# Routing-weight scaling of the experts' transposed results: from ScalarE and SyncE's queue to Pool

## The chip, the core and the metric

The kernel runs on one core of a Trainium2 chip. Its engines run side by side: TensorE (PE in the profile, with its weight loads as PEld), VectorE (DVE), ScalarE (ACT), GpSimd (POOL) and SyncE (SP), which only asks for DMA transfers. Each engine takes its instructions in order; semaphores order engines against each other. The metric is the device time of one execution in microseconds; the median of several runs is given.

## The reference, cut to what matters

Each of 8 batches of 256 tokens is first multiplied by the adapter matrix chosen for it. A mixture-of-experts layer follows: a shared feed-forward network for all tokens, and 16 experts of which each token uses its two best, weighted. The result is added to the input.

```python
x1 = einsum('bsi,boi->bso', x, weight[adapter_ids])           # 2048 tokens x 1024
shared_out = (silu(g_s) * u_s) @ shared_w_down.T              # g_s, u_s = split(x1 @ shared_w_gate_up.T)
probs = softmax(x1 @ gate_w.T)                                # 16 experts
topk_vals, topk_idx = top_k(probs, 2)                         # divided by their sum -> combine
act = silu(g) * u                                             # g, u = split(x1 @ w_gate_up[e].T), 256 each
moe_out = sum over e of (act_e @ w_down[e].T) * combine[:, e]
out = x + moe_out + shared_out
```

Everything is float32. The change touches the multiplication by `combine`.

## The kernel before, in words

**Products.** Float32 matrices are split into a high part (fp32r, a cast on ScalarE, L88) and the rest (a subtraction on VectorE, L89), and each product is three matmuls (`mm3`, L139 to L141): high by high, high by rest, rest by high. Weights are loaded by SP into a staging tile `st` (four buffers), and split into `hl` (five buffers, and two more in the experts' stage), by `load_w` (L119).

**Stages.** The kernel computes the adapters' products for all batches, the first half of the shared network and the routing (to about 440 us), then the experts (about 440 to 740 us), then the second half of the shared network with the final sums. The routing sorts the tokens of each expert into a list; experts are run in order of their load, counted here from 0. Expert n has room for `CAPS[n]` tokens: 304, 296, 288, 288, 280, 280, 272, 272, 264, 264, 264 for the first eleven, and 256 for the last five. A rarely needed loop at the end handles tokens beyond that.

**One expert.** Pool gathers its tokens' rows from memory, 128 rows of 1 KB per request (L839): eight requests into two `yg` tiles (four buffers, so two experts' worth), and one or two into the small tile `yl`. VectorE transposes them (L226) into `tt`, and they are split into `yte`. PE computes gate and up (`expert_up`), ScalarE the silu (L865), VectorE the product with up (L866), and the result is split into `at`. Then PE computes the down product.

**The down product of the first eleven.** Where an expert has more than 256 tokens, `expert_down_columns` has PE produce the result turned, with features on partitions: eight blocks of 128 features by all tokens, each in a bank of its own (seven banks `acc` go round). ScalarE copies each block into the tile `raw[0]` (L920, 88 copies). VectorE turns it with two 32x32 block transposes into `raw[1]` (L922). There, partition 32a + i holds, for token 32t + i, the features 256a to 256a + 255, for each of the `nt` groups of 32 tokens (`nt` is 10 for the first two experts and 9 for the nine after them). ScalarE multiplies each group by the token's weight, a value per partition from `cwt[:, t, n]` (L928). SP asks for four stores to `os_d`, each of 32 partitions by `nt` pieces of 1 KB (L936). `raw[0]` and `raw[1]` are single buffers: the next expert's copies wait for this expert's transposes, and the next expert's transposes wait for this expert's stores. The last five experts use `expert_down`, whose copy out of the bank already scales (L895).

**The order of the work.** The order of instructions on each engine comes from a scheduler that follows the program's order and its own estimate of times. The program steers it with a list `between`: `load_w` takes one entry after each weight load, and the entry's instructions are placed after that load's split. The main loop calls, for each n: the gathers of expert n+2, `expert_up` of n+1 (four loads), `expert_out` of n (two loads, then the down product), and the transposes and splits of n+2. An expert's scaling is thus spread over the fourth, fifth and sixth load after its down product. On SP, a store that waits holds back the weight loads behind it.

Of the kernel before, what the change touches and what calls it, by code (L numbers as in the profile page):

```python
# [13 lines left out]
AF = mybir.ActivationFunctionType  # L14
ALU = mybir.AluOpType
AX = mybir.AxisListType

P = 128
# [23 lines left out]
def adapter_moe_kernel(ctx: ExitStack, tc: tile.TileContext, xT, x, itok, wc, gate, wgu, wd, sgu, sd, out):  # L42
    nc = tc.nc
# [35 lines left out]
    def bank():  # L79
        turn[0] += 1  # L80
        return banks[turn[0] % 7]

    last_cast, last_split, last_load = [None], [None], [None]
# [17 lines left out]
    between = []  # L101
# [36 lines left out]
    def mm3(ps, lhs, rhs, first, last):  # L138
        nc.tensor.matmul(ps, lhs[0], rhs[0], start=first, stop=False)  # L139
        nc.tensor.matmul(ps, lhs[0], rhs[1], start=False, stop=False)  # L140
        last_product[0] = nc.tensor.matmul(ps, lhs[1], rhs[0], start=False, stop=last).ins  # L141
# [32 lines left out]
    cwt = cpool.tile([P, ENTRIES // 32, 32], F32, tag="cwt", name="cwt")  # L174
# [730 lines left out]
    def expert_down_columns(n, at, w):  # L905
        m, rows, nt = CAPS[n], ROWS[n], ROWS[n] // 32
        ot, o = (r[:, :, :].rearrange("p c n -> p (c n)") for r in raw)
        ot = ot[:, : 8 * rows].rearrange("p (b t i) -> p b t i", b=8, i=32)
        o = o[:, : nt * 256].rearrange("p (t f) -> p t f", t=nt)
        for b in range(8):  # L910
            ps = bank()
            for fi in range(2):
                mm3(
                    ps[:, :m],
                    [w[fi][:, l, b * P : (b + 1) * P] for l in range(2)],
                    [at[:, l, fi, :] for l in range(2)],
                    fi == 0,
                    fi == 1,
                )
            nc.scalar.copy(ot[:, b], ps[:, :rows].rearrange("p (t i) -> p t i", i=32))  # L920
        for k in range(2):
            nc.vector.transpose(o[:, :, k * P : (k + 1) * P].rearrange("p t (b j) -> p b t j", b=4), ot[:, 4 * k : 4 * k + 4])  # L922

        def scaled(ts, end):
            def work():
                with tc.issue_after(last_cast[0]):
                    for t in range(nt)[ts]:
                        nc.scalar.activation(o[:, t], o[:, t], AF.Copy, scale=cwt[:, t, n : n + 1])  # L928
                if end:
                    store()  # L930

            return work

        def store():
            for a in range(4):
                nc.sync.dma_start(  # L936
                    os_d[ROW0[n] : ROW0[n] + rows, 256 * a : 256 * a + 256].rearrange("(t i) f -> i t f", i=32),
                    o[32 * a : 32 * a + 32],
                )

        between[:] = [None, None, None, scaled(slice(0, 3), False), scaled(slice(3, 6), False), scaled(slice(6, nt), True)]


    def segments(ix, ib):
# [45 lines left out]
    def expert_out(po, n, at):  # L990
        w = load_wd(expert_id(n))
        if CAPS[n] > MAIN:
            expert_down_columns(n, at, w)
            return
        for j in range(2):
            (nc.gpsimd if n > 13 else nc.sync).dma_start(os_d[ROW0[n] + j * P : ROW0[n] + (j + 1) * P, :], expert_down(po, at, w, j * P, cw[:, j, n : n + 1]))
# [32 lines left out]
    op = up.begin_work()  # L1029
# [186 lines left out]
    for n in range(E):  # L1216
# [14 lines left out]
        if n + 1 == E:  # L1231
# [3 lines left out]
            op = up.begin_work()  # L1235
# [163 lines left out]
```

## Time and profile before

| | us |
|---|---|
| median of 3 runs | 982.19 (979.61 to 986.2) |
| profiled execution | 981.36 |
| its span, from first to last instruction | 979.2 |
| PE busy | 962.2 |
| VectorE busy | 715.3 |
| ScalarE busy | 558.6 |
| of that, the scaling (L928, 101 x 497 ns) | 41.6 |
| Pool busy | 309.2 |
| of that, the gathers of rows into `yg` (L839, 128 x 1213 ns) | 155.2 |

Busy time is the time in which an engine executed an instruction; DMA requests count as busy on Pool, but not on SP. In a row of instruction groups stand the line, the engine, the operation, what it writes and reads, the count, then busy time and mean nanoseconds of one, then the idle time ahead of these instructions and what ended it. A row of a timeline has the start, the duration, the instructions, and in brackets the idle time before them.

### The profile page before, as it was taken

To read this page: it belongs to the slowest core of one execution; us is meant where nothing else is said; L and a number is where in the kernel's file an instruction comes from. 1 tells how busy PE (TensorE), PEld (TensorE's weight loads), DVE (VectorE), ACT (ScalarE), POOL (GpSimd) and SP (SyncE) were. 2 spreads that over 40 slices of the span, in tenths; PEclk is the share of its full clock that TensorE was granted. 3 is DMA by queue.
4 is the path that set the end of the run, shared out by engine and by line. 5 is a ranking of instruction groups with operands and counts; after the bars stand their busy time and mean duration, and the time that the engine had idled before them with its cause. 6 is when DMAs were issued, how large, how long until landed. Compare 5 with 4: busy or idle time off the path is not lost.

```text
span 979.2 us, 14565 instructions
## 1 busy us (share of the span) xinstructions
PE 962.2 (98%) x5183; PEld 834.5 (85%) x5183; DVE 715.3 (73%) x908; ACT 558.6 (57%) x819; POOL 309.2 (32%) x336
## 2 busy tenths in 40 slices
PE   8999999999999999999979999999999999999997
PEld 5888888888888888889969999999998888888886
DVE  4566888864779678649967888887878565969772
ACT  5556746566645452325758888878765465425440
POOL 2000200100074103666745556552001433330600
PEclk9999999999999999999979999999999999999999
DMA  8899967977799746868869989999997998994942
GB/s 299 283 322 356 372 209 278 370 252 246 247 213 259 164 126 134 295 233 260 243 221 286 309 279 287 299 308 321 310 328 263 326 355 310 272 263 127 250 147 100
DMA packets 92741, 257.62 MB, mean 263 GB/s; under 512 B 13298, under 2 KB 32514, under 8 KB 92658
## 3 DMA queue, kind: packets, MB, share of 16 engines
q1 hardware_dynamic: 60002, 173.04, 54.4%
q0 software_dynamic: 23056, 73.98, 23.9%
q10 hardware_dynamic: 9600, 9.57, 2.8%
q8 instruction: 42, 0.69, 0.3%
q14 instruction: 41, 0.34, 0.1%
HBM read 207.62 MB, written 48.93 MB: 262 GB/s over the span
## 4 chain that ended last, share of the span: by engine, by line
PE 94%; DMA 2%; issue 1%; DVE 1%; ACT 1%; SPq 0%; ACTq 0%
PE acc L530 31%; PE acc L141 19%; PE acc L139 19%; PE acc L140 19%; PE acc L731 5%; PE lp L286 1%; DMA st<-sd 1%; DMA st<-wc 1%; ACT hl L88 0%; DVE hl L89 0%; DVE shl L89 0%; ACT op L88 0%; DVE ca L759 0%; SPq L114 0%; DVE st L798 0%
## 5 line engine op out<-in xcount | busy, mean ns | idle before, releaser
L89 DVE TENSOR_TENSOR hl<-st,hl 128x1024 fp32r<-128x1024 f32 (+1 forms) x254 | 304.9, 1208 | 174.4 <-ACT hl L88 143.4
L88 ACT CAST hl<-st 128x1024 fp32r<-128x1024 f32 (+1 forms) x254 | 263.5, 1044 | 192.2 <-PE acc L141 70.6
L530 PE MATMUL acc<-op,hl 128*128 128x512 f32 x1296 | 298.0, 390 | 0.0
L530 PEld LDWEIGHTS acc<-op,hl 128*128 128x128 f32 x1296 | 242.4, 188 | 50.2
L839 POOL DMA_INDIRECT yg<-y_d,ix x128 | 155.2, 1213 | 80.1 <-issue 33.9
L141 PE MATMUL acc<-yte,hl 128*128 128x256 f32 (+6 forms) x512 | 147.2, 288 | 0.4 <-issue 0.4
L140 PE MATMUL acc<-yte,hl 128*128 128x256 f32 (+6 forms) x512 | 147.1, 287 | 0.3 <-issue 0.3
L139 PE MATMUL acc<-yte,hl 128*128 128x256 f32 (+6 forms) x512 | 147.3, 289 | 0.0
L140 PE MATMUL acc<-hl 128*128 128x512 f32 x256 | 100.3, 392 | 0.9 <-DVE hl L89 0.7
L141 PE MATMUL acc<-hl 128*128 128x512 f32 x256 | 99.7, 390 | 0.0
L141 PEld LDWEIGHTS acc<-yte,hl 128*128 128x128 f32 x512 | 96.3, 188 | 0.4 <-issue 0.4
L140 PEld LDWEIGHTS acc<-yte,hl 128*128 128x128 f32 x512 | 96.4, 188 | 0.2
L139 PEld LDWEIGHTS acc<-yte,hl 128*128 128x128 f32 x512 | 96.3, 188 | 0.2
L139 PE MATMUL acc<-hl 128*128 128x512 f32 x256 | 90.4, 391 | 1.5 <-ACT hl L88 1.5
L140 PEld LDWEIGHTS acc<-hl 128*128 128x128 f32 x256 | 48.0, 188 | 12.9 <-DVE hl L89 3.0
L139 PEld LDWEIGHTS acc<-hl 128*128 128x128 f32 x256 | 47.7, 188 | 12.3 <-ACT hl L88 2.5
L386 POOL DMA_INDIRECT tab_d<-tid,places x32 | 39.8, 1244 | 56.3 <-DVE ranks L372 46.8
L141 PEld LDWEIGHTS acc<-hl 128*128 128x128 f32 x256 | 48.1, 188 | 9.8
L139 PE MATMUL acc<-at,hl 128*128 128x264 f32 (+5 forms) x176 | 52.6, 299 | 2.7 <-issue 2.1
L141 PE MATMUL acc<-at,hl 128*128 128x264 f32 (+5 forms) x176 | 52.0, 295 | 2.5 <-issue 2.5
L140 PE MATMUL acc<-at,hl 128*128 128x264 f32 (+5 forms) x176 | 52.4, 298 | 1.3 <-issue 1.3
L141 PE MATMUL acc<-hl,ht 128*128 128x512 f32 x128 | 50.0, 391 | 0.0
(234 smaller groups left out, 1454.6 us busy)
## 6 DMA issues: line engine op xcount, KB each, us to landing
st<-wgu SPq DMA_DIRECT2D x64, 512.0 KB
st<-wc SPq DMA_DIRECT2D x63, 512.0 KB
st<-wd SPq DMA_DIRECT2D x32, 512.0 KB
st<-ss_d SPq DMA_DIRECT2D x30, 512.0 KB
st<-sd SPq DMA_DIRECT2D x30, 512.0 KB
st<-sgu SPq DMA_DIRECT2D x24, 512.0 KB
os_d<-raw SPq DMA_DIRECT2D x36, 288.0 KB
yr<-y_d POOLq DMA_DIRECT2D x20, 512.0 KB
```

The lines of the kernel that those rows point to most:

```text
L88: last_cast[0] = nc.scalar.copy(hi, src).ins
L89: last_split[0] = nc.vector.tensor_tensor(lo, src, hi.bitcast(F32), op=ALU.subtract).ins
L139: nc.tensor.matmul(ps, lhs[0], rhs[0], start=first, stop=False)
L140: nc.tensor.matmul(ps, lhs[0], rhs[1], start=False, stop=False)
L141: last_product[0] = nc.tensor.matmul(ps, lhs[1], rhs[0], start=False, stop=last).ins
L286: nc.tensor.matmul(lp[:, n0 : n0 + n], gpk[:, c * 2 * E : c * 2 * E + P], get(c)[l], start=(c == 0 and l == 0), stop=(c == NC - 1 and l == 1),
L386: i = nc.gpsimd.indirect_dma_start(out=tab_d[:, :], out_offset=bass.IndirectOffsetOnAxis(ap=places[r][:, tb : tb + 1], axis=0), in_=tid[r] ...
L530: last_product[0] = nc.tensor.matmul(ps, lhs[x], rhs[y], start=(first and c == 0 and i == 0), stop=(c == 3 and i == 2), skip_group_check=T ...
L731: nc.tensor.matmul(ps[k], lhs[x], rhs[y], start=(first and t == c == i == 0), stop=(t == c == 1 and i == 2), skip_group_check=True,)
L839: last_gather[0] = nc.gpsimd.indirect_dma_start(out=r[:, t * 256 : (t + 1) * 256], out_offset=None, in_=y_d.rearrange("k a p f -> (k a p) f"),
```

## The change

The three entries of `between` that scaled groups of 32 tokens on ScalarE become one entry, after the fourth load. It issues a single product on Pool: the whole of `raw[1]`, 128 partitions by `nt` x 256, times the weights spread over the 256 features by a stride of zero. The four stores are issued directly behind it by Pool instead of SP. Work, values and tiles are otherwise the same.

```diff
-        def scaled(ts, end):
-            def work():
-                with tc.issue_after(last_cast[0]):
-                    for t in range(nt)[ts]:
-                        nc.scalar.activation(o[:, t], o[:, t], AF.Copy, scale=cwt[:, t, n : n + 1])
-                if end:
-                    store()
-
-            return work
-
-        def store():
+        def scaled():
+            by = cwt[:, :nt, n : n + 1].to_broadcast([P, nt, 256])
+            nc.gpsimd.tensor_tensor(o, o, by, op=ALU.mult)
             for a in range(4):
-                nc.sync.dma_start(
+                nc.gpsimd.dma_start(
                     os_d[ROW0[n] : ROW0[n] + rows, 256 * a : 256 * a + 256].rearrange("(t i) f -> i t f", i=32),
                     o[32 * a : 32 * a + 32],
                 )
 
-        between[:] = [None, None, None, scaled(slice(0, 3), False), scaled(slice(3, 6), False), scaled(slice(6, nt), True)]
+        between[:] = [None, None, None, scaled]
```

Pool's instructions stand in one order with its gathers. In the changed program's order the first product stands behind the gathers of expert 5, the product of expert 3 behind those of expert 9, that of expert 6 behind those of expert 12, and that of expert 7 behind those of expert 14; between a product and its stores there are often one to five gathers. On VectorE the two transposes of an expert stand together and later than before, close to the point where the next expert's copies begin.

## The prediction

> **What bounds the kernel now.** I read the page first: busy shares, then the chain that ended last.
>
> ```profile
> PE 962.2 (98%) x5183; PEld 834.5 (85%) x5183; DVE 715.3 (73%) x908; ACT 558.6 (57%) x819; POOL 309.2 (32%) x336
> PE 94%; DMA 2%; issue 1%; DVE 1%; ACT 1%; SPq 0%; ACTq 0%
> ```
>
> TensorE is the bound: 98% busy, 94% of the chain. A change that relieves another engine can win only PE's idle time; one that makes another engine late costs at once. Pool's 32% is an average over stages, so next I read the experts' stage by stretches. The columns are PE, PEld, DVE, ACT and POOL busy, granted clock, DMA share and GB/s.
>
> ```profile
> 552.00:571.00 19.00, 19.00 (x152) 19.00 (x151) 16.31 (x19) 15.96 (x32) 11.16 (x10) 1.00 0.90 291
> 571.00:590.00 19.00, 19.00 (x153) 19.00 (x152) 16.05 (x19) 15.35 (x31) 10.25 (x10) 1.00 0.86 293
> 487.00:669.00 182.00, 174.76 (x1352) 172.75 (x1351) 149.06 (x165) 143.54 (x276) 102.83 (x87) 0.97 0.87 283
> ```
>
> One expert takes about 19 us and PE has no gap in it. PE's 7.2 us of idle time in the third row lie almost wholly at 489-500 and are put down to "issue", not to ScalarE. Next, Pool in time order, since the work goes there:
>
> ```profile
> 561.92 0.95 POOL L839 DMA_INDIRECT yl<-y_d,ix  x1 [3.52 <-DVE tt L226]
> 565.07 1.86 POOL L839 DMA_INDIRECT yg<-y_d,ix  x1 [2.19 <-DVE yte L89]
> 567.24 0.96 POOL L839 DMA_INDIRECT yg<-y_d,ix  x1 [0.30 <-issue]
> ...
> 575.74 0.96 POOL L839 DMA_INDIRECT yg<-y_d,ix  x1 [0.30 <-issue]
> 580.15 0.95 POOL L839 DMA_INDIRECT yl<-y_d,ix  x1 [3.46 <-DVE tt L226]
> 584.26 1.80 POOL L839 DMA_INDIRECT yg<-y_d,ix  x1 [3.16 <-DVE yte L89]
> ```
>
> Eight gathers run back to back with 0.30 us between them, then one small gather. Pool's free time per expert is only the two waits for buffers. Over 487-669 it is 182 - 102.8 busy - 87 x 0.30 = 53 us, or 5.6 us per expert of 19.1 us.
>
> Last, the chain around the change, for experts 4 and 5 (experts count from 0), from the timelines of ACT, SP and DVE:
>
> ```profile
> 567.43 3.72 ACT L928 ACTIVATE raw<-raw,cwt 128x256 f32<-128x256 f32 x9
> 571.23 4.11 SPq L936 DMA_DIRECT2D os_d<-raw  x4
> 577.79 0.69 ACT L920 COPY raw<-acc 128x288 f32<-128x288 f32 x2
> 581.49 1.38 DVE L922 STREAM_TRANSPOSE raw<-raw 128x1152 f32<-128x1152 f32 x1 [1.28 <-DMA os_d<-raw]
> 585.15 1.37 DVE L922 STREAM_TRANSPOSE raw<-raw 128x1152 f32<-128x1152 f32 x1
> ```
>
> This is a ring through two single buffers. Expert n's transposes fill the second raw tile; scaling and stores empty it; only then may expert n+1's transposes start, which here already waited 1.28 us. Expert n+2's copies (L920) in turn need the first raw tile that those transposes read, and PE needs the copies to free its banks.
>
> **The change, part by part.** *Removed:* 101 activations,
>
> ```profile
> L928 ACT ACTIVATE raw<-raw,cwt 128x256 f32<-128x256 f32 x101 | 41.6, 497 | 3.9 <-DVE raw L922 3.8
> ```
>
> 41.6 us of ScalarE. Beside a full PE they are worth nothing directly: the page's waits of PE on ACT are 1.5 and 0.7 us. I take 0, at most 2 us. The 44 store requests also leave SP's queue (about 4 us per expert ahead of the next weights); PE shows no wait for weights in this stage, so 0 again.
>
> *Added on Pool, the product.* There are eleven, nine of 128x2304 and two of 128x2560. No row shows a Pool product of two inputs. The nearest is a write alone:
>
> ```profile
> L218 POOL MEMSET zr<- 128x1024 f32 x1 | 1.0, 957 | 4.6 <-DVE raw L226 4.6
> ```
>
> 0.957 / 1024 x 2304 = 2.15 us is the low end. The Trainium skill (GPSIMD Engine Reference, Performance versus the Vector engine) has 4497 ns for a two-input float add over 2048 elements a partition, because both inputs come through one read port. That gives an estimate of 5.06 us for 2304 and 5.62 for 2560. The memset reads nothing, so I take the page's value and keep 2.15 as the other end. With the gap of 0.30 it is 5.4 us (5.9 for the first two).
>
> *Added on Pool, the four stores.* Each is 32 partitions x 9 pieces of 1 KB = 288 pieces. Near rows: Pool's plain 128-piece loads (yr from y_d) take 0.55 us, and its 128x4-piece writes to y_d take
>
> ```profile
> L280 POOL DMA_DIRECT2D y_d<-yrow x4 | 3.2, 790 | 34.6 <-ACT yrow L278 34.6
> ```
>
> so between them 0.65 us; up to 1.21, an indirect gather's mean. Four with gaps: 4 x 0.95 = 3.8 us (3.3 to 6.0).
>
> *Sum.* Pool per expert: 8 x (1.213 + 0.30) + 1.25 = 13.4 us now, 22.5 us after, against PE's 19. The extra 9.2 us does not fit the 5.6 free ones. Nine products and their stores stand before the last expert's gathers in the changed program: 2 x 9.7 + 7 x 9.2 = 84 us, less 53 free, so Pool reaches the end of its gathers 30 us later even if it never idles. The gathers alone could bear that (the last ones end at 668 and their rows are transposed at 689-692). The ring cannot, since Pool is in order and products and stores stand between gathers of far later experts.
>
> *The order and the walk.* In the changed instruction order expert 3's product follows expert 9's eight gathers; expert 3's stores follow another small gather and four of expert 10's; expert 6's product follows expert 12's gathers, and expert 7's follows all of 14's. I walk Pool from 487.4 (where the first product comes up) with 1.51 us a gather, 1.25 a small one, the prices above, 2.8 us for the two transposes, and 4 us from the last store request to its landing. That last is an estimate: the stores took 10.3 us from first request to landing on SP's ring (571.23 to 581.49) behind two weight loads; alone on Pool's ring, 1.18 MB at half of 291 GB/s is 8 us, less the 3.8 of requests.
> - Expert 3: gathers end 568, product 573.4, stores asked for until 584.5, landed 588.5, expert 4's transposes done 591.3. Expert 5's copies began at 577.8 before: 13.5 us late.
> - Expert 4: product 603.2, stores 613.0, expert 5's transposes done 619.8; copies of 6 at 596.1 before: 23.7 late.
> - Expert 5 (next to its stores): transposes of 6 done 637.0, copies of 7 at 614.6: 22.4.
> - Expert 6: product 647.7, stores 657.5, transposes of 7 done 664.3, copies at 633.9: 30.4.
> - Expert 7: product 681, stores 684.8, 691.6 against 652.4: 39.
> - Expert 8: product 697, stores 706.8, transposes of 9 done 713.6, copies of 10 at 669.2: 44.4.
> PE may run about 4 us ahead into free banks (some five of seven, 0.8 us each), so about 40 us of delay stay. Experts 11 to 15 don't use the ring and keep it. What is queued behind these waits: DVE's splits of weights stand behind the waiting transposes, ScalarE's casts behind the waiting copies, so the split weights dry up with them.
>
> *The shared port.* The Trainium skill (SBUF — State Buffer, Who interferes with whom) says a VectorE instruction with two SBUF inputs and a Pool instruction that reads SBUF shut each other out for a whole instruction. VectorE's commonest one is such:
>
> ```profile
> L89 DVE TENSOR_TENSOR hl<-st,hl 128x1024 fp32r<-128x1024 f32 (+1 forms) x254 | 304.9, 1208 | 174.4 <-ACT hl L88 143.4
> ```
>
> By the trace alone the product costs VectorE nothing (Pool has no such instruction beside it now). By the rule it takes up to 5.1 us from an engine that is busy 16.2 of 19: 21.3 us, over PE's 19 but under Pool's 22.5. So I count it at 0 in the likeliest case; it decides only where Pool is faster than I think.
>
> Total: span 979.2 + 40 = 1019; 2.2 us lie outside the span (profiled execution 981.36), and the median of the runs is 0.8 above that one: 1022 us.
>
> **The rivals.**
> *Pool absorbs it (not slower).* If the product streams at the memset's pace (2.15) and a store costs 0.53, the extra is 2.45 + 4 x 0.83 = 5.8 us per expert, just Pool's free 5.6, and the ring closes in time. This decides below about 5.7 us extra, so a product under about 1.6 us with my store price or 2.1 with the cheapest. Then nothing is late, ScalarE's relief is worth 0 to 2 us: 980 to 984. For it: gathers have some 20 us of lead. Against it: the port rule and the page's 4497. Chance 0.15.
> *The lock bites both ways.* Products wait for splits in flight (up to 1.2 us) and splits for products, and stores cost up to 1.2 us: 9 x (1.2 + 2.2) = 31 us more, 1053. Chance 0.16.
> *A shorter product in the same ring.* Halfway to the low end, 1.5 us less times nine: about 1008; it belongs to the main case.
> *PE's stall at 489-500 moves.* 7 us of idle and as many at half clock (granted 0.50 at 494-502) are put down to issue; another instruction stream might miss them, some 10 us, 971, if Pool also absorbs everything. Chance 0.05.
>
> **How the numbers follow.** Main case 0.64, about 995 to 1050: the low end of the product takes 2.9 x 9 = 26 off, dear stores add 20. The range of 8 in 10 reaches down into the absorbed case and stops at the lock's centre: 984 to 1053. A measurement of this kernel can't tell less than 1% (10 us) from no change. Faster by over 1%: 0.05. Within: 0.15. Slower: 0.80.
>
> **What would show it.** Pool's busy share in 540-700 at 0.9 or more with gaps; products of about 5 us; L922 waiting for os_d stores over 5 us per expert; L920 waiting for L922; PE gaps of several us per expert between 575 and 715 with granted clock below 1; the last third unchanged. Wrong if products take near 2 us, or if VectorE's splits are stretched while Pool stands idle.

## The result, and the profile after

The changed kernel takes 1040.5 us (median of 4 runs, 1035.4 to 1050.6) against 982.3 us of the kernel before beside it (979.6 to 986.2): the ratio is 1.060, 95% interval 1.055 to 1.065. It is slower by 58 us. The profiled execution has a span of 1038.8 us (979.2 before).

The page of the changed kernel, busy shares and the chain that ended last:

```profile
PE 977.6 (94%) x5183; PEld 848.0 (82%) x5183; DVE 751.5 (72%) x908; ACT 519.7 (50%) x718; POOL 384.3 (37%) x391
PE 62%; POOL 13%; issue 9%; DMA 8%; DVE 5%; ACT 2%; SPq 0%; DVEq 0%; ACTq 0%; POOLq 0%
```

TensorE's share of the chain fell from 94% to 62%, and Pool, which was not on the chain at all, has 13%. VectorE, whose work the change leaves alone, is busy 36 us longer (751.5 against 715.3): that is the first sign of the shared port, which the prediction counted at nothing in its likeliest case.

Where the 58 us lie is read from the stretches. Columns: stretch and its length, busy us (and instructions) of PE, PEld, DVE, ACT and POOL, granted clock, DMA share, GB/s. First the whole experts' stage, before:

```profile
487.00:740.00 253.00, 245.76 (x1854) 239.64 (x1853) 205.47 (x223) 194.79 (x357) 107.57 (x96) 0.98 0.88 292
```

and after, with two single turns below it:

```profile
487.00:798.00 311.00, 258.30 (x1849) 250.38 (x1848) 241.52 (x222) 160.08 (x265) 185.49 (x151) 0.92 0.70 238
...
611.00:630.00 19.00, 13.16 (x85) 12.93 (x84) 12.70 (x10) 9.24 (x17) 7.30 (x4) 0.82 0.42 151
...
706.00:725.00 19.00, 9.19 (x63) 8.97 (x62) 12.68 (x14) 8.93 (x17) 13.42 (x13) 0.78 0.82 304
```

The stage is 58 us longer (311 against 253); what precedes 487 us and what follows the experts (240.8 us against 239.2) is nearly unchanged. PE is idle for 52.7 us of it (311 - 258.3), 7.2 before: 45.5 us more. The other 12.5 us are PE's own busy time. It grew with a lower granted clock, 0.82 and 0.78 in the two stretches with stalls shown above: busy time times clock is 241 us before (245.76 x 0.98) and 238 after (258.30 x 0.92), so the clock accounts for the growth.

What PE waits for, from the waits of the stage (total us, times, longest):

```profile
PE acc L139 <- ACT raw L920: 43.3, 6, 9.8
POOL raw L927 <- DVE raw L922: 39.9, 5, 11.2
DVE raw L922 <- DMA os_d<-raw: 31.9, 8, 7.6
...
ACT raw L920 <- DVE raw L922: 24.5, 5, 8.7
```

That is the ring, read as a chain: the stores' landing holds the transposes (L922), the transposes hold ScalarE's copies (L920) *and* the product (L927), and the copies hold PE. One turn of it in time order, Pool's timeline for experts 4 and 5 (start, us, instruction; in brackets the idle time before it):

```profile
598.47 4.07 POOL L927 TENSOR_TENSOR raw<-raw,cwt 128x2304 f32<-128x2304 f32 x1
602.70 1.78 POOL L839 DMA_INDIRECT yg<-y_d,ix  x1 [0.16 <-issue]
604.78 1.96 POOL L839 DMA_INDIRECT yg<-y_d,ix  x1 [0.30 <-issue]
607.05 1.16 POOL L839 DMA_INDIRECT yg<-y_d,ix  x1 [0.30 <-issue]
608.51 0.96 POOL L839 DMA_INDIRECT yg<-y_d,ix  x1 [0.30 <-issue]
609.47 2.54 POOL L929 DMA_DIRECT2D os_d<-raw  x4
622.79 4.94 POOL L927 TENSOR_TENSOR raw<-raw,cwt 128x2304 f32<-128x2304 f32 x1 [10.77 <-DVE raw L922]
```

The product ends at 602.5, but its stores stand behind four gathers of a much later expert and are asked for from 609.5. They land when VectorE's timeline shows the next transposes released, 8.1 us after the last request (620.06 against 612.01). The next instruction in Pool's order is the product that waits for these transposes, so Pool idles for 10.8 us. VectorE's timeline of the same stretch:

```profile
598.32 7.59 DVE L89 TENSOR_TENSOR hl<-st,hl 128x1024 fp32r<-128x1024 f32 x3 [0.70 <-ACT hl L88]
...
620.06 2.64 DVE L922 STREAM_TRANSPOSE raw<-raw 128x1152 f32<-128x1152 f32 x2 [5.65 <-DMA os_d<-raw]
622.62 1.18 DVE L89 TENSOR_TENSOR yte<-tt,yte 128x1024 fp32r<-128x1024 f32 x1
623.73 4.29 DVE L89 TENSOR_TENSOR at<-s,at 128x272 fp32r<-128x272 f32 x1
```

Two things beside the ring are to be seen. Three weight splits that start with the product of 598.47 take 7.59 us in place of some 3.7. And a small split of 128x272, which takes 0.43 us elsewhere in this stretch, takes 4.29: it starts after the product of 622.79 and ends after it.

### The profile page after: what moved, and what is told of

It is laid out like the page before. It is cut to its first block, busy times and chain, and to the rows that moved or that the text cites. A ratio compares the mean times of both kernels' runs of the same rounds, so it can differ in the third digit from the quotient of the medians.

```text
span 1038.8 us, 14446 instructions
## 1 busy us (share of the span) xinstructions
PE 977.6 (94%) x5183; PEld 848.0 (82%) x5183; DVE 751.5 (72%) x908; ACT 519.7 (50%) x718; POOL 384.3 (37%) x391
## 4 chain that ended last, share of the span: by engine, by line
PE 62%; POOL 13%; issue 9%; DMA 8%; DVE 5%; ACT 2%; SPq 0%; DVEq 0%; ACTq 0%; POOLq 0%
PE acc L530 30%; POOL yg L839 9%; PE acc L140 8%; PE acc L141 8%; PE acc L139 8%; PE acc L731 7%; DMA os_d<-raw 3%; POOL raw L927 2%; DMA st<-wgu 2%; DVE hl L89 2%; POOL os_d L929 2%; PE lp L286 1%; DVE yte L89 1%; ACT hl L88 1%; DMA yg<-y_d,ix 1%
## 5 line engine op out<-in xcount | busy, mean ns | idle before, releaser
L89 DVE TENSOR_TENSOR hl<-st,hl 128x1024 fp32r<-128x1024 f32 (+1 forms) x254 | 321.2, 1274 | 176.9 <-ACT hl L88 160.0
L139 PE MATMUL acc<-yte,hl 128*128 128x256 f32 (+6 forms) x512 | 151.9, 298 | 0.0
L140 PE MATMUL acc<-yte,hl 128*128 128x256 f32 (+6 forms) x512 | 151.4, 296 | 0.0
L141 PE MATMUL acc<-yte,hl 128*128 128x256 f32 (+6 forms) x512 | 151.2, 296 | 0.0
L139 PE MATMUL acc<-at,hl 128*128 128x264 f32 (+5 forms) x176 | 54.5, 309 | 49.9 <-ACT raw L920 43.3
L139 PEld LDWEIGHTS acc<-yte,hl 128*128 128x128 f32 x512 | 101.2, 198 | 0.2
L140 PEld LDWEIGHTS acc<-yte,hl 128*128 128x128 f32 x512 | 101.2, 198 | 0.2
L141 PEld LDWEIGHTS acc<-yte,hl 128*128 128x128 f32 x512 | 100.7, 197 | 0.0
L139 PEld LDWEIGHTS acc<-at,hl 128*128 128x128 f32 x176 | 34.5, 196 | 52.9 <-ACT raw L920 44.6
L927 POOL TENSOR_TENSOR raw<-raw,cwt 128x2304 f32<-128x2304 f32 (+1 forms) x11 | 48.4, 4398 | 40.0 <-DVE raw L922 39.9
L386 POOL DMA_INDIRECT tab_d<-tid,places x32 | 37.4, 1170 | 57.9 <-DVE ranks L372 48.5
L89 DVE TENSOR_TENSOR yte<-tt,yte 128x1024 fp32r<-128x1024 f32 (+6 forms) x43 | 53.9, 1275 | 2.2 <-ACT yte L88 2.2
```

Of the source, the lines that this page charges most:

```text
L89: last_split[0] = nc.vector.tensor_tensor(lo, src, hi.bitcast(F32), op=ALU.subtract).ins
L386: i = nc.gpsimd.indirect_dma_start(out=tab_d[:, :], out_offset=bass.IndirectOffsetOnAxis(ap=places[r][:, tb : tb + 1], axis=0), in_=tid[r] ...
L927: nc.gpsimd.tensor_tensor(o, o, by, op=ALU.mult)
```

## The experiments

Two causes are on the table after the comparison, and two simpler stories. *Ring:* one raw tile is filled, scaled, stored and landed in turn, and two of these steps now stand in Pool's order behind gathers. *Port:* the product shuts VectorE's splits out. *Stores:* asking for them from Pool is by itself the harm. *Pool's time:* Pool is simply full, as the prediction had it. Line numbers shift by a few between these kernels; the operation names don't. Each kernel has a short name, under which later texts refer to it. Ratios are those to the kernel before beside each run: it took 981.2 us (median) beside `stores_only`, `product_only`, `two_memsets` and `gathers_behind`, 972.9 beside `memsets_sp`, `gathers_behind_stores`, `pieces_sp` and `one_input_sp`, and 981.8 beside the other four.

**Each half of the change alone.** The stores on Pool, the scaling left on ScalarE (`stores_only`):

```diff
-                nc.sync.dma_start(
+                nc.gpsimd.dma_start(
```

> The kernel before, with the four stores of each expert asked for by Pool and the scaling left on ScalarE. The ring theory (transposes, scaling, stores and landing close through one raw tile, and a step of it stands in Pool's order behind gathers): part of the loss, 1000 to 1025 us, since the stores stand behind gathers but the product does not delay them. The stores theory (their move to Pool's queue does all of it): 1035 to 1045. The port theory (the product's shared port stretches VectorE's splits): no product, so 980 to 985.

Measured: 985.4 us, ratio 1.006 (1.003 to 1.008). The stores' move costs some 5 us by itself, so the stores theory falls. The ring theory was also too high. The profiled execution is a long one (997.5 us), but its delay lies ahead of the experts' stage: between 400 and 450 us PE is idle for 7.7 us, at a granted clock of 0.90, where the kernel before has no gap. The waits of the stage tell why the cost is small:

```profile
DVE raw L922 <- DMA os_d<-raw: 12.2, 6, 3.5
...
PE acc L139 <- ACT raw L920: 7.0, 5, 2.1
```

The same waits appear, but short. Only one step of the ring, the stores, stands behind gathers now; the reading is that the slack of a turn covers most of it.

The product on Pool, the stores left on SP (`product_only`, an edit of the kernel after):

```diff
-                nc.gpsimd.dma_start(
+                nc.sync.dma_start(
```

> The kernel after, with the four stores of each expert asked for by SP as before; the product stays on Pool. Ring theory: the product still stands behind gathers in Pool's order, the stores follow it at once on SP: most of the loss, 1015 to 1035 us. Stores theory: 980 to 990. Port theory: all of it, 1035 to 1045, with the hl splits at 1430 ns in the experts' stage as in the kernel after.

Measured: 1022.3 us, ratio 1.041 (1.032 to 1.050). The number is inside the ring's range, but the profile shows other causes, which makes the expectation right for the wrong reason. PE hardly waits for L920 any more (1.5 us); it waits for VectorE's product with up (L866):

```profile
PE acc L139 <- DVE s L866: 26.7, 12, 4.4
```

VectorE's weight splits in 487-740, from the groups by form (count, busy, mean ns, idle before):

```profile
L89 DVE TENSOR_TENSOR hl<-st,hl 128x1024 fp32r<-128x1024 f32 x66 | 112.6, 1718 | 7.3 <-ACT hl L88 6.4 <-issue 0.8
```

From the waits of SP's queue in the stage:

```profile
SPq L929 <- POOL raw L927: 16.2, 3, 7.8
```

A split takes 1718 ns (1207 before). And SP, in order like the others, stood 16.2 us before stores whose product wasn't done, with weight loads queued behind them: ScalarE waited 48.2 us for weights, 24.4 before.

**The port taken out.** In the kernel after, the product is replaced by two writes of the same tile (`two_memsets`), which hold Pool about as long (2 x 2.03 us) and read nothing; the scaling by the weights is left out:

```diff
-            nc.gpsimd.tensor_tensor(o, o, by, op=ALU.mult)
+            for r in range(2):
+                nc.gpsimd.memset(o, 1.0)
```

> The kernel after, with two Pool memsets of the same tile in place of each product (the scaling by the weights is left out): Pool is held about as long (2 x 2.15 us against 4.1 to 4.9) at the same place of the ring, but reads nothing. Ring theory: as the kernel after, 1030 to 1042 us, at most the 0.8 us less per expert that a product loses to splits. Port theory: the splits fall back to about 1210 ns in the experts' stage and the time to 985 to 1005.

Measured: 1014.3 us, ratio 1.036 (1.028 to 1.045), between the two expectations, so neither theory alone has it. The weight splits of the stage, by form:

```profile
L89 DVE TENSOR_TENSOR hl<-st,hl 128x1024 fp32r<-128x1024 f32 x68 | 82.3, 1215 | 44.1 <-ACT hl L88 34.3 <-issue 4.9 <-ACT s L865 2.8
```

And from the waits of the stage:

```profile
PE acc L139 <- ACT raw L920: 18.8, 4, 7.4
```

The splits are back at 1215 ns, so it is the product's reading that stretches them, as the Trainium skill states (SBUF — State Buffer, Who interferes with whom: a VectorE instruction with two SBUF inputs contends with a Pool instruction that reads SBUF, not with one that only writes). VectorE's busy time is 717.6 us, the value of before within 2.3. What is left, some 36 us, is the ring without the port, though not in quite the same order: as there are two instructions in place of one, the scheduler put gathers between them in some turns. In the longest case, between these two, there are four:

```profile
631.14 2.02 POOL L928 MEMSET raw<- 128x2304 f32 x1 [9.77 <-DVE raw L922]
639.64 2.04 POOL L928 MEMSET raw<- 128x2304 f32 x1
```

In all eleven turns 26 gathers stand between the start of the writes and the stores, 24 in the kernel after, but in other turns. So the difference of 26 us between this kernel and the kernel after is not the port's alone.

The same with the stores on SP (`memsets_sp`):

> The kernel after, with two Pool memsets of the tile in place of each product (the scaling is left out) and the stores asked for by SP. Pool's work and its place in the order are those of product_only within 0.5 us, but Pool reads nothing. Port theory: the hl splits stay at about 1215 ns in the experts' stage and the 41 us of product_only are gone, 980 to 990 us. Order theory (the product's wait behind gathers alone does it): as product_only, 1015 to 1025.

Measured: 998.9 us, ratio 1.027 (1.023 to 1.030), again between. The splits take 1206 ns, and PE waits only 6.2 us for L920; what stays is a cost that no theory had named. From the waits of SP's queue:

```profile
SPq L930 <- POOL raw L928: 24.9, 9, 6.4
```

and from those of the engines:

```profile
ACT hl L88 <- DMA st<-wgu: 62.2, 18, 10.2
```

SP waits 24.9 us for Pool, and ScalarE 62.2 us for weights queued behind it (5.6 us with the stores on Pool, in `two_memsets`). So moving the stores to Pool along with the scaling does remove a real wait: left on SP, they block the weight loads. On Pool they stand behind gathers instead. This kernel is no clean counterpart of `product_only` either: in six of its turns up to four gathers stand between the two writes, so the place in the order that the expectation took to be equal is not.

**The order on Pool.** In the kernel after, the gathers of later experts are issued behind the last product (`gathers_behind`):

```diff
+            last_scaled.append(nc.gpsimd.tensor_tensor(o, o, by, op=ALU.mult).ins)
...
-            rs = expert_rows(pa[1], n + 2)
+            with tc.issue_after(last_scaled[-1]) if last_scaled else nullcontext():
+                rs = expert_rows(pa[1], n + 2)
```

> The kernel after, with the gathers of later experts put behind the last product in the order, so that a product no longer stands behind the gathers of an expert six further on. Theory that Pool's order makes the ring late: the product follows its transposes at once, L927's wait remains short, 985 to 1010 us, the rest of the loss being the 8 us of landing and the port. Port theory: the products are still eleven and still beside splits, 1035 to 1045. Theory that Pool lacks the time (22 us of work against PE's 19): 1030 to 1045 as well, with Pool busy throughout.

Measured: 1067.3 us, ratio 1.086 (1.075 to 1.098), worse than every expectation. The edit moved the gathers from ahead of the product to between the product and its stores, and Pool's timeline gives the ring's period plainly:

```profile
597.23 4.05 POOL L928 TENSOR_TENSOR raw<-raw,cwt 128x2304 f32<-128x2304 f32 x1 [7.89 <-DVE raw L923]
601.44 1.84 POOL L840 DMA_INDIRECT yg<-y_d,ix  x1
...
613.52 2.54 POOL L930 DMA_DIRECT2D os_d<-raw  x4
625.08 4.05 POOL L928 TENSOR_TENSOR raw<-raw,cwt 128x2304 f32<-128x2304 f32 x1 [9.02 <-DVE raw L923]
```

One turn is the product 4.1, nine gathers and their gaps 12.2, the requests 2.5, landing and transposes 9.0: 27.85 us (625.08 - 597.23). From 542.96 to 738.87 us seven turns take 195.9 us, 28.0 each. PE needs 19. Eleven experts at 9 us too much would be 99; 86 were measured. Pool idles in every turn, so its time is not what is short.

The same edit with the stores ahead of the gathers as well (`gathers_behind_stores`: the gathers come behind the last store request):

> The kernel after, with the gathers of later experts put behind the last expert's stores (not only behind its product as in gathers_behind). Ring theory: one turn is transposes 2.6, product 4.1, stores 2.5, landing 8 = 17 us, below the 19 us of an expert, so the ring no longer sets the pace and what is left is the port: as product_only, 1010 to 1025 us. If the gathers then come too late because they wait for the stores: 1035 to 1070 with VectorE's tt transposes waiting for yg.

Measured: 995.0 us, ratio 1.021 (1.017 to 1.025), better than expected and with everything that the change moves still on Pool. Its timeline:

```profile
607.47 4.07 POOL L928 TENSOR_TENSOR raw<-raw,cwt 128x2304 f32<-128x2304 f32 x1
611.83 2.56 POOL L930 DMA_DIRECT2D os_d<-raw  x4 [0.30 <-POOL raw L928]
614.69 1.43 POOL L840 DMA_INDIRECT yg<-y_d,ix  x1 [0.30 <-issue]
...
628.21 4.07 POOL L928 TENSOR_TENSOR raw<-raw,cwt 128x2304 f32<-128x2304 f32 x1
```

Pool hardly idles here, and eight products follow each other in 161 us (524.43 to 685.45), 20.1 us each. That is eight gathers, a small one, a product and four stores in 20.1 us, where the prediction had put 22.5. PE's wait for L920 is 3.7 us. The splits are as long as ever (1535 ns in the stage): the port is in this kernel, the late ring is not. But a third thing is in it now: Pool, without idle time, needs 20.1 us for an expert and PE about 19.

The fourth corner, this order with two writes in place of the product (`memsets_gathers_behind_stores`; here the writes and the stores stand together in every turn):

> gathers_behind_stores with two memsets in place of each product (the scaling is left out): the order in which the ring closes in time, and nothing that reads through the shared port. Two-cause theory (ring 33 us in two_memsets, port 21 us in gathers_behind_stores, 58 together): neither is left, within 5 us of the kernel before. If Pool's load itself, or the later gathers, cost something: 10 us or more stay.

Measured: 991.4 us, ratio 1.009 (1.006 to 1.012). It missed the 5 us; 9 stay. With it the four corners are complete (ratio to before):

| | after's order on Pool | gathers behind the stores |
|---|---|---|
| product (reads SBUF) | 1.060 (1.055 to 1.065) | 1.021 (1.017 to 1.025) |
| two writes of the tile | 1.036 (1.028 to 1.045) | 1.009 (1.006 to 1.012) |

So the order, and with it the ring, costs 2.7 points where Pool only writes and 3.9 where it reads, 27 to 38 us of 982 (23 and 46 in plain microseconds). The port is known less well. The left column gives 2.4 points, but its two kernels differ in their order, as said above. The right column is a clean pair and gives 1.2 points, 12 us; but its upper corner is the one measured beside a kernel before of 972.9 us. In plain microseconds the two are 995.0 and 991.4, so the port costs 4 to 12 us where the ring is in time. That it costs more in a late ring is likely and not shown.

The 9 us of the last corner were not expected. Pool's own pace is a candidate that no run tested. Its timeline, at both ends of eight turns:

```profile
521.74 4.13 POOL L929 MEMSET raw<- 128x2304 f32 x2
...
681.38 4.10 POOL L929 MEMSET raw<- 128x2304 f32 x2 [4.70 <-DVE raw L923]
```

That is 20.0 us a turn, with next to no idle time until the last. At about 1 us more than PE needs, nine turns come to some 9 us (an estimate from these two figures). Measured from the first copies (L920) of expert 1 to those of expert 10, these nine experts take 177.7 us here, 182.6 with the product and 166.8 before. The last gathers into `yg` start at 711.7 us here and at 715.0 with the product, against 666.4 before. So of the 22 us of `gathers_behind_stores`, too, a part may be Pool's time and not the port.

**The tile.** If the ring closes because one tile serves every expert, a second tile opens it without moving anything off Pool (`two_tiles`). Its 10 KB come from one of the seven buffers of split weights; `after_pw1` gives up that buffer and nothing else:

```diff
-        ot, o = (r[:, :, :].rearrange("p c n -> p (c n)") for r in raw)
+        ot = raw[0][:, :, :].rearrange("p c n -> p (c n)")
+        o = second[0][:, :] if n % 2 else raw[1][:, :, :].rearrange("p c n -> p (c n)")
...
-    pw = pool("pw", 2, "right")
+    pw = pool("pw", 1, "right")
+    second.append(pb[1].tile([P, 2560], F32, tag="second", name="second"))
```

> The kernel after, with every second expert's transposes, product and stores in a second tile of 10 KB a partition; the room comes from one of seven buffers of the split weights. If the ring closes through the one tile: two experts per turn, so the wait of L922 for the stores goes and only the port is left, 1000 to 1015 us. If what is late is Pool's order and not the tile: 1030 to 1050. Read against after_pw1, which gives up the same buffer.

> The kernel after, with six buffers of split weights instead of seven and nothing else changed: what the room for a second tile costs by itself. 1038 to 1055 us by every theory.

Measured: 1003.5 us with the second tile, ratio 1.019 (1.014 to 1.025); 1020.2 us for the kernel with six buffers and no second tile, ratio 1.039 (1.036 to 1.043). The second tile is worth 2.0 points, some 17 to 20 us, at equal buffers. That giving up a buffer made the changed kernel *faster* by 2 points was not expected. The waits of that second kernel show that it is the same ring:

```profile
PE acc L139 <- ACT raw L920: 19.1, 5, 8.1
...
DVE raw L922 <- DMA os_d<-raw: 3.3, 4, 1.3
```

With six buffers the order comes out differently: the stores of experts 1 to 6 follow their products with no gather into `yg` between, where the kernel after has four in several turns. The landing wait fell from 31.9 to 3.3 us and PE's from 43.3 to 19.1. So the order on Pool decides what the change costs, and it is not fixed by the change.

The second tile in the worst order, that of `gathers_behind` (`gathers_behind_two_tiles`):

> gathers_behind with the second tile of two_tiles. Ring theory: gathers_behind turned once in 27 to 29 us by its products; with two tiles that is 14 us per expert, under PE's 19, so its 86 us fall to what the port takes, 1000 to 1020 us. If its loss was the gathers' lateness: 1050 or more.

Measured: 1000.2 us, ratio 1.019 (1.015 to 1.023). The gathers are still ahead of the stores and every product still on Pool, but the loss of 8.6 points falls to 1.9, about that of `gathers_behind_stores`. Of PE's wait for L920, 53.2 us in `gathers_behind`, 0.2 us is left in the stage. So in this order the late ring through the one tile was the cause; what is left is again the port and a Pool with hardly any idle time.

**The port in small pieces.** The product in nine (ten) instructions of 128x256, and a scaling with one tensor input and a scalar for each partition, both with the stores on SP (`pieces_sp` and `one_input_sp`, so against `product_only`):

```diff
-            nc.gpsimd.tensor_tensor(o, o, by, op=ALU.mult)
+            for t in range(nt):
+                nc.gpsimd.tensor_tensor(o[:, t], o[:, t], by[:, t], op=ALU.mult)
```

> product_only with the same product in nine (ten) Pool instructions of 128x256. If the harm is that a split waits for one whole long instruction: splits wait at most some 0.5 us each, 985 to 1000 us. If the two engines just share out the port's time: the sum of what they need is unchanged, 1010 to 1025.

```diff
-            nc.gpsimd.tensor_tensor(o, o, by, op=ALU.mult)
+            for t in range(nt):
+                nc.gpsimd.tensor_scalar(o[:, t], o[:, t], cwt[:, t, n : n + 1], None, op0=ALU.mult)
```

> product_only with the product written as nine (ten) Pool instructions of one 128x256 input and a scalar for each partition. If any Pool instruction that reads SBUF shuts VectorE's splits out: about as product_only, 1010 to 1025 us, the splits longer than 1300 ns. If only two inputs do it: 980 to 995, the splits at about 1215 ns.

Measured: 1038.0 us (ratio 1.067, 1.063 to 1.071) and 1049.0 us (1.077, 1.072 to 1.081), both above both expectations. The pieces (min, median and max ns of one, first and last start):

```profile
L928 POOL TENSOR_TENSOR raw<-raw,cwt x101: 602/1552/1595, 488.8 to 739.2; 128x256 f32<-128x256 f32 x101
```

and the weight splits of the stage, by form:

```profile
L89 DVE TENSOR_TENSOR hl<-st,hl 128x1024 fp32r<-128x1024 f32 x62 | 80.2, 1307 | 1.6 <-ACT hl L88 1.6
```

A piece that takes 0.60 us at the least mostly takes 1.55, as if it waited out a split. The splits grow by only 0.1 us in the mean (the longest takes 1.67). Now Pool loses: 120.0 us for what took 48.4 in the kernel after, and SP waits 63.5 us for it. Small pieces turn most of the port's cost from VectorE to Pool; here that is the worse side. The other kernel answers its question badly, because Pool's own price came in between:

```profile
L928 POOL TENSOR_SCALAR raw<-raw,cwt x101: 912/967/2961, 487.6 to 771.7; 128x256 f32<-128x256 f32 x101
```

One of 256 elements takes 0.97 us (median; 1.4 in the mean, so 12.6 us for nine); the ring is late from that alone (PE waits 56.3 us for L920). The weight splits took 1253 ns in it, little more than before, but whether one tensor input blocks less than two, or only short instructions do, stays open.

## Why the prediction was right or wrong

The sign, the place and the main mechanism, a ring made late by Pool's order, held: 1022 was predicted, 1040.5 measured, inside the range. That the number came within 18 us is in part luck, as errors of both signs stand in its parts. Step by step:

- *PE is the bound, and ScalarE's relief is worth 0 to 2 us:* held. ScalarE's busy time fell by 39 us, and no variant with the product on Pool came below the kernel before.
- *The walk of the ring:* held, closer than its parts deserved. Products were to end at 573.4, 603.2, 647.7, 681 and 697 for experts 3, 4, 6, 7 and 8; they ended at 571.7, 602.5, 649.2, 681.4 and 699.8. Stores were to be asked for until 584.5, 613.0, 657.5 and 706.8; measured 585.2, 612.0, 661.6 and 710.6. The order of instructions on Pool carried these numbers.
- *Landing, 4 us after the last request:* mis-sized, half of what was measured. It is 8.1 us for expert 4, 7.9 to 8.9 in the turns of experts 3, 7 and 8 (for instance 684.2 to 692.14). The prediction had put 8 us from the first request to the landing and taken the requests off; from the first request it is 10.6 us for expert 4.
- *Product, 5.06 us:* 4.07 us for 128x2304 and 4.50 for 128x2560 where no split was in flight, 4.94 where one was. The Trainium skill's price (GPSIMD Engine Reference, Performance versus the Vector engine) was the nearer end, as chosen, but 24% above this case's 4.07.
- *Stores, 3.8 us:* 2.54. Four plain store requests follow each other without the 0.30 us gap that the indirect gathers have between them. Product and stores together came 2.5 us cheaper per turn than predicted, landing 4 dearer; the errors largely cancelled in the walk.
- *Pool's period of 22.5 us against PE's 19, Pool busy 0.9 and more in 540-700:* wrong. Pool was busy 108.3 of those 160 us, 0.68, and idle for 39.9 us of the stage, waiting for transposes. It does one expert's work in 20.1 us when nothing holds it (gathers_behind_stores). The ring set the pace in this kernel; Pool's period would have been the milder limit, and may be one in `gathers_behind_stores`.
- *The shared port, counted at 0:* wrong. The prediction reasoned that VectorE at 21.3 us per expert stays under Pool's 22.5, so the lock is hidden behind Pool. Pool was not the limit, and a stretched split delays what stands behind it on VectorE: the products with up that PE waits for in `product_only` (26.7 us), and the transposes. VectorE was busy 36 us longer. How much of that is in the 18 us between 1022 and 1040.5 stays open: 4 to 12 us by the clean pair of corners, and the pair in the order of the kernel after is not clean.
- *PE's clock:* the walk had no term for it. PE's busy time in the stage grew by 12.5 us with the granted clock at 0.92; no run separates it from the stalls beside which it shows.
- *The walk's end:* "about 40 us stay" was taken at expert 8, with expert 10's copies 44.4 us late. They were 53 late by the transposes that release them (722.1 against 669.2), and the products of experts 9 and 10 came at 722.2 and 740.3 with the ring still late.

The rivals: *Pool absorbs it* fell (product 4.07, not under 2.1). *The lock bites both ways* was half right: it bit VectorE, while the product lost only 0.9 us in some turns and the stores were cheap. *A shorter product in the same ring* came true as a part without its effect, since landing took the gain (4 us dearer against 2.5 cheaper). *PE's stall moves* came true, though no kernel came below the kernel before: from 490 to 500 us PE is busy for 9.96 us at a granted clock of 1.00, against 4.28 at 0.64 before, and expert 1's first copies begin 9 us earlier (493.2 against 502.4). The ring takes more than that back: from there to expert 10's copies it is 227.7 us, against 166.8. So the net 58 us hide a loss of some 61 us and a gain of 9, which the main case had left out.

## What to carry to other kernels

Before moving a step onto another engine's queue, write down the ring that it closes (every step from filling a buffer to its release, landing included) in that queue's real order, and compare one turn with the bound's time per item; an engine with free time can still close a ring late, and a second buffer or a better place in the order can then be worth more than a faster step. A long two-input Pool instruction such as this product, beside a VectorE full of two-input operations, has to be charged to VectorE too. When both halves of a change are cheap or explicable alone, run the corners: here the stores alone cost 0.6 points, the product alone 4.1, both 6.0, and the order on Pool alone moved that between 2.1 and 8.6. When an instruction is replaced by others that keep an engine as busy, check that they also keep its order.

## What the runs showed of the hardware that was not expected

- A split and a product wait for each other about one instruction at a time, as far as these rows show. A 128x272 split took 4.29 us in place of 0.43 under one long product, and a 128x256 piece of the product 1.55 us in place of 0.60 beside the splits; VectorE's one-input transposes of 128x1024 (1.23 us in the stage of `gathers_behind_stores`, 1.22 before) and Pool's writes (2.03 us) showed nothing of it.
- Of some 35 us by which the product stretched VectorE's work (750.6 against 715.3 us in `gathers_behind_stores`), only 4 to 12 reached the time where the ring was in time: VectorE had 48 us of idle time in that stage in the kernel before (253 - 205.5).
- Pool's price depends on the form. The product with a spread second operand took 1.77 ns per element (4.07 us for 2304). Of 128x256 it took 0.60 us at the least; with one input and a scalar for each partition, the same size took 0.91 at the least and 0.97 in the median.
- Four plain stores of 1.18 MB together, asked for by Pool in 2.5 us, landed 7.9 to 8.9 us after the last request in the kernel after.
